# VectorE's order in the edge loop of a graph network: the add of an edge part between the two products of an older unit

## The chip, the cores and the metric

The kernel runs on one core of one Trainium2 chip. The time is that of one execution on the device, in microseconds (us), as the median of several runs. A profile of one more execution gives the rows quoted below. TensorE is PE in those rows (its weight loads are PEld), VectorE is DVE, ScalarE is ACT, GpSimd is POOL, SyncE is SP.

## The reference

One layer of a graph network on 6250 nodes with 256 features and 206250 edges (100000 pairs in both directions, and one loop for each node), sorted by target node. All data are fp32.

```python
h = relu(layernorm(x))                                   # no gain or bias here
polarity = clip(edge_attr[:, 0:1], 0, 1)
e = relu(edge_attr[:, 1:] @ W_e1.T + b_e1) @ W_e2.T + b_e2
edge_emb = (e * (polarity + 0.01)) @ W_le.T + b_le
msg = relu(h[src] + edge_emb)
aggr = segment_sum(msg, dst)
g = (h + aggr) @ W_g1.T + b_g1
out = x + relu(layernorm(g) * ln_g + ln_b) @ W_g2.T + b_g2
```

## The kernel before, in words

The host only lays the arrays out. A first phase normalises x and writes h + b_le to memory in HBM (`hb_d`). It also multiplies W_e2 by W_le into one matrix (`wc_s`, with the offset `bc_s`), so that each edge needs two matrix products: the first layer, and the edge part.

The edges go in **blocks** of 512 (403 of them), a block in two **units** of 256 edges (NU = 806 units, `u`), and two blocks, that is four units, in a **turn** (some 201). The program is written out in full, without a loop on the chip: Python loops place the instructions of each engine in the order in which they are issued, and no scheduler moves them. Every engine runs its own list in order and waits at semaphores for the others.

`forward(u)` places unit u:

- `edge_part(u)`: eight matmul records on TensorE (L326) into a PSUM bank `pz`, and then, on VectorE, the **add** (L332) `msg[u] = pz + bc_s`, which frees the bank. There are seven such banks, taken in a ring by all steps that need one; the matmul that takes a bank again waits for its last reader.
- in each unit with `u % 4 == 1`, `turn_of`: the **first layer** (L293) of the turn two further on, into four banks, which three relus on ScalarE (L309) and one operation on VectorE (L306) read; then the **sums** (L696), in which 0/1 matrices `sel` add the finished messages of a turn by target node on TensorE.

After `forward(u)` the loop over units places on VectorE one **piece** (`piece()`: a part of a `sel` matrix, L656, or a step of the node work, L793 or L231), and then the **products** of an older unit, `whole(made)`: for each half i of the unit `hg = msg * polarity + hg` (L678), where `hg` holds the rows of h that GpSimd gathered from `hb_d` (an indirect DMA, L627). A relu on ScalarE (L683) over the whole unit follows, and `hg` is then ready for the sums. How far `made` trails u is set by `lag`: 18 units at first, fewer as the loop goes on. In a unit with `u % 4 == 0` the lag is one larger, so that no product stands in it, and in the one after it, `u % 4 == 1`, two units' products do, behind the first layer. This holds for all but the first and last six turns (`by_two`).

After that, `due()` places at most one step of the **node work** in a unit with `u % 4` of 2 or 3: for each of the 49 windows of 128 nodes a transpose, a matrix product whose bank VectorE reads (L190), a layer normalisation (L152, L153, L158, L194), a second transpose that ScalarE reads (L204), a last product and the output (L218). ScalarE's L171 reads the first transpose.

`gathers(n)` places gathers up to unit n where they aren't placed yet; most are placed earlier, in step with TensorE, by `paced`. `add_pairs`, called as `sums`, places as many turns of sums as `made` allows, with three units (`LATER`) kept in between.

## Time and profile before

| | |
|---|---|
| median of three runs | 2539.52 us (2538.93 to 2548.43) |
| profiled execution | 2536.68 us, span 2534.7 us |
| TensorE busy | 2300.1 us, 91% of the span |
| VectorE busy | 1606.2 us, 63% |
| ScalarE busy | 1004.0 us, 40% |
| GpSimd busy | 1657.5 us, 65% |
| DMA | 330.25 MB, mean 130 GB/s |

A row of a group reads: line, engine, operation, written tile <- read tiles, shape, count | busy us, mean ns of one | idle us of the engine directly before such instructions, and what ended most of that. A row of waits reads: engine, tile and line that waited <- what ended the wait: us in total, times, the longest. A row of the timeline reads: start in us, us, the instruction, how many of them, and in brackets the idle time before it and what ended it. "issue" and "remote" stand for a wait whose end the profile shows no releaser for. A row of a window reads: its us, then busy us and count of PE, PEld, DVE, ACT and POOL, the granted clock of TensorE, the DMA share, and GB/s.

### The profile page before, as it was taken

How to read it: one execution, taken by the hardware profiler on the slowest of the kernel's cores; microseconds unless marked ns; L12 is line 12 of the kernel's file. 1: busy time of each engine (PE TensorE's matmuls, PEld its weight loads, DVE VectorE, ACT ScalarE, POOL GpSimd, SP SyncE). 2: the span in 40 equal slices, each digit the busy share in tenths (PEclk: the TensorE clock that was granted, in tenths of full speed). 3: DMA queues.
4: the chain of work that ended last, by engine and by line, in shares of the span. 5: the costliest groups of instructions: out<-in, count | busy, mean ns of one | idle time of the engine just before them, and what ended most of it. 6: DMA issues, size and time to landing. Idle time of an engine off the chain costs nothing.

```text
span 2534.7 us, 36092 instructions
## 1 busy us (share of the span) xinstructions
PE 2300.1 (91%) x11940; PEld 1573.7 (62%) x11940; DVE 1606.2 (63%) x3705; ACT 1004.0 (40%) x1804; POOL 1657.5 (65%) x1675
## 2 busy tenths in 40 slices
PE   9988999999989999899999999999999999899967
PEld 6665666566656666666666666666656666656645
DVE  7876666656666666566656665666666666656645
ACT  7433343333433344333434343334343433433422
POOL 7666666666666666666666666666666666666661
PEclk9999999999999999999999999999999999999988
DMA  9444443444444344444444444344444444443441
GB/s 309 140 122 134 132 129 116 127 137 124 129 129 131 116 131 135 133 119 127 136 132 130 118 129 136 116 127 137 130 122 128 133 136 121 129 133 116 119 125 38
DMA packets 176425, 330.25 MB, mean 130 GB/s; under 512 B 39056, under 2 KB 98281, under 8 KB 176233
## 3 DMA queue, kind: packets, MB, share of 16 engines
q0 software_dynamic: 77376, 211.39, 29.8%
q1 hardware_dynamic: 97556, 113.22, 13.8%
q10 hardware_dynamic: 1300, 3.28, 0.4%
q8 instruction: 95, 1.56, 0.3%
q14 instruction: 98, 0.79, 0.1%
HBM read 293.92 MB, written 33.82 MB: 129 GB/s over the span
## 4 chain that ended last, share of the span: by engine, by line
PE 81%; DVE 8%; issue 7%; another core or an unknown queue 2%; ACT 1%; DMA 0%; DVEq 0%; ACTq 0%; POOL 0%; POOLq 0%
PE pz L326 55%; PE pz L293 14%; PE pd L696 8%; DVE hg L678 2%; DVE msg L332 2%; PE pz L213 2%; PE pz L182 2%; DVE sel L656 1%; DVE st L152 0%; PE pz L167 0%; PE pz L200 0%; DVE e L306 0%; ACT hg L683 0%; ACT xt L433 0%
## 5 line engine op out<-in xcount | busy, mean ns | idle before, releaser
L627 POOL DMA_INDIRECT hg<-hb_d,src_s x1604 | 1612.6, 1005 | 808.3 <-issue 506.8
L326 PE MATMUL pz<-wc_s,e 128*128 128x256 f32 x6448 | 1578.8, 394 | 134.2 <-issue 120.9
L326 PEld LDWEIGHTS pz<-wc_s,e 128*128 128x128 f32 x6448 | 1235.2, 196 | 448.2 <-issue 236.7
L332 DVE TENSOR_TENSOR msg<-pz,bc_s 128x512 f32<-128x512 f32 x799 | 543.0, 686 | 733.2 <-PE pz L326 297.1
L683 ACT ACTIVATE hg<-hg 128x512 f32<-128x512 f32 x805 | 501.0, 629 | 997.9 <-DVE hg L678 827.0
L678 DVE SCALAR_TENSOR_TENSOR hg<-msg,pol_s,hg 128x256 f32<-128x256 f32 x1612 | 690.5, 478 | 10.1 <-DMA hg<-hb_d,src_s 5.3
L309 ACT ACTIVATE e<-pz,vecs 128x512 f32<-128x512 f32 x605 | 373.3, 684 | 243.4 <-remote 111.6
L293 PE MATMUL pz<-raw,we_s 64*128 64x512 f32 x1612 | 420.1, 626 | 40.2 <-DVE msg L332 24.9
L293 PEld LDWEIGHTS pz<-raw,we_s 64*128 64x128 f32 x1612 | 137.3, 186 | 223.3 <-issue 132.5
L696 PE MATMUL pd<-hg,sel 128*32 128x256 f32 x3216 | 241.0, 391 | 26.2 <-issue 25.3
L306 DVE TENSOR_SCALAR e<-pz,vecs 128x512 f32<-128x512 f32 x201 | 149.8, 745 | 137.9 <-remote 47.6
L696 PEld LDWEIGHTS pd<-hg,sel 128*32 128x32 f32 x3216 | 91.0, 110 | 226.9 <-issue 180.7
L656 DVE SCALAR_TENSOR_TENSOR sel<-iota_w,zero_c,rel 128x128 f32<-128x128 f32 x403 | 138.3, 343 | 0.0
L711 ACT ACTIVATE ms<-pd 128x256 f32<-128x256 f32 x66 | 25.4, 385 | 243.6 <-PE pz L326 101.6
L182 PE MATMUL pz<-wg_s,hT 128*128 128x256 f32 (+1 forms) x196 | 53.5, 387 | 12.3 <-issue 11.1
L213 PE MATMUL pz<-wg_s,nT 128*128 128x256 f32 (+1 forms) x196 | 51.5, 384 | 2.7 <-issue 1.8
L182 PEld LDWEIGHTS pz<-wg_s,hT 128*128 128x128 f32 (+1 forms) x196 | 37.0, 191 | 20.0 <-issue 13.1
L213 PEld LDWEIGHTS pz<-wg_s,nT 128*128 128x128 f32 (+1 forms) x196 | 37.2, 191 | 8.3 <-issue 2.1
L437 POOL TENSOR_TENSOR hb<-xt,rows_b 128x256 f32<-128x256 f32 (+1 forms) x49 | 34.1, 729 | 10.4 <-ACT xt L433 4.4
L204 ACT ACTIVATE nT<-pz,vecs 128x128 f32<-128x128 f32 (+1 forms) x98 | 38.8, 445 | 2.4 <-PE pz L200 2.4
L793 DVE TENSOR_TENSOR stb<-stb,ab 128x256 f32<-128x256 f32 x94 | 39.2, 417 | 0.0
L231 DVE SCALAR_TENSOR_TENSOR xt<-xt,zero_c,rows_b 128x128 f32<-128x128 f32 (+1 forms) x98 | 33.6, 344 | 0.0
(108 smaller groups left out, 379.9 us busy)
## 6 DMA issues: line engine op xcount, KB each, us to landing
raw<-in_raw_t_dram SPq DMA_DIRECT2D x202, 256.0 KB
hg<-hb_d,src_s POOLq DMA_INDIRECT x1604
sum_d<-zrow SPq DMA_DIRECT2D x94, 128.0 KB
ab<-sum_d SPq DMA_DIRECT2D x94, 128.0 KB
sum_d<-ms SPq DMA_DIRECT2D x264, 32.0 KB
hb_d<-hb SPq DMA_DIRECT2D x12, 512.0 KB
xt<-in_x_dram SPq DMA_DIRECT2D x48, 128.0 KB
out_dram<-ot SPq DMA_DIRECT2D x48, 128.0 KB
```

Source lines behind the costliest of these rows:

```text
L182: z = nc.tensor.matmul(ph[:n, 0, :], aT[:, c, :n], wg1_s[:, c, :], start=c == 0 and not bias_by_pe, stop=c == 1)
L213: z = nc.tensor.matmul(po[:n, 0, :], nT[:, c, :n], wg2_s[:, c, :], start=c == 0, stop=c == 1)
L293: z[c] = nc.tensor.matmul(pe[s, c], we1_s[s * F:(s + 1) * F, c * P:(c + 1) * P], raw[q][s * F:(s + 1) * F, :], start=True, stop=True)
L306: a = nc.vector.tensor_scalar(e1[b][:, c, :], pe[s, c], be1_s[:, c:c + 1], 0.0, op0=ALU.add, op1=ALU.max)
L309: a = nc.scalar.activation(e1[b][:, c, :], pe[s, c], AF.Relu, bias=be1_s[:, c:c + 1])
L326: last_z = nc.tensor.matmul(pz[:, i, :], e1[b][:, c, k:k + P], wc_s[:, c, :], start=c == 0, stop=c == 1)
L332: ps.read(nc.vector.tensor_add(msg[u], pz, bc_s))
L627: g = nc.gpsimd.indirect_dma_start(out=hg[u][:, i, :], out_offset=None, in_=hb_d, in_offset=bass.IndirectOffsetOnAxis(ap=src_s[:, 2 * u + ...
L656: nc.vector.scalar_tensor_tensor(sel[g][:, k * S:(k + 1) * S, :], iota_w.rearrange("p (o w) -> p o w", o=1).to_broadcast([P, S, W]), zero_ ...
L678: product = nc.vector.scalar_tensor_tensor(hg[u][:, i, :], m[:, i, :], pol_s[:, 2 * u + i:2 * u + i + 1], hg[u][:, i, :], op0=ALU.mult, op ...
L683: done[u] = product, nc.scalar.activation(hg[u], hg[u], AF.Relu)
L696: z = nc.tensor.matmul(acc[g][j * W:(j + 1) * W, :], sel[g][:, k * S + j, :], m[:, j % 2, :], start=k == 0, stop=b == blocks_of(g)[-1])
```

## The change

The add of unit u is placed between the two products of the older unit that is due in the same step of the loop (`half_of_products`, called ahead of the add and behind it). Before, both products came after the add, after a first layer where there is one, and after a piece. Only one older unit per step is split in this way (`eager`), and only where `by_two` holds. The second unit in a step with `u % 4 == 1` keeps its place behind the first layer, and `whole` now takes one more piece between its two products. The sums count as if the eager unit weren't made yet, so that they take the same turns as before.

```diff
@@ edge_part
             msg[u] = msg_p.tile([P, 2, D], F32, name="msg")
+            half_of_products(u, 0)
             if plain(u):
                 ps.read(nc.scalar.activation(msg[u], pz, AF.Copy))
             else:
                 ps.read(nc.vector.tensor_add(msg[u], pz, bc_s))
+            half_of_products(u, 1)
@@
-            def whole(u):
-
-                m = msg.pop(u)
+            def products(u, i):
+
+                if i == 0:
+                    opened(u)
+                product = nc.vector.scalar_tensor_tensor(hg[u][:, i, :], msg[u][:, i, :], pol_s[:, 2 * u + i:2 * u + i + 1],
+                                               hg[u][:, i, :], op0=ALU.mult, op1=ALU.add)
+                if u == NU - 1:
+                    nc.scalar.activation(hg[u][:, i, :], hg[u][:, i, :], AF.Relu)
+                elif i == 1:
+                    done[u] = product, nc.scalar.activation(hg[u], hg[u], AF.Relu)
+                if i == 1:
+                    msg.pop(u)
...
+            def whole(u, between=lambda: None):
+
+                products(u, 0)
+                between()
+                products(u, 1)
@@ add_pairs
-                while summed + pairs < NP and min(4 * (summed + pairs) + 4, NU) < made + last - (0 if last or summed > NP - 2 * FEW else LATER):
+                while summed + pairs < NP and min(4 * (summed + pairs) + 4, NU) < made - eager + last - (0 if last or summed > NP - 2 * FEW else LATER):
@@
+            def due_at(u):
+
+                lag = max(LEAST, LEAD - RAW - u // SHRINK) + (by_two(u // 4) and (u + 1) % 4 == TURN)
+                return min(u + 1 - lag, 5 * (u + 1 - LEAD) // 4)
+
+            def half_now(u, i):
+
+                nonlocal made, eager
+                if i == 0:
+                    eager = by_two(u // 4) and made < due_at(u)
+                    if eager:
+                        gathers(made + 1)
+                if eager:
+                    products(made, i)
+                    made += i
@@ the loop over units
-                lag = max(LEAST, LEAD - RAW - u // SHRINK) + (by_two(u // 4) and (u + 1) % 4 == TURN)
-                ready_for = min(u + 1 - lag, 5 * (u + 1 - LEAD) // 4)
-                while made < ready_for:
+                while made < due_at(u):
                     gathers(made + 1)
-                    whole(made)
+                    whole(made, piece)
                     made += 1
```

The lists of TensorE, GpSimd and SyncE keep their order from first to last; VectorE's and ScalarE's change. Below, an add is the row that writes `msg`, a product one that writes `hg` from `msg`, and the number in a name tells tiles apart (it differs between the two programs for the same tile). Line numbers shift: L332, L678, L656 and L683 of before are L333, L677, L659 and L682 after.

VectorE in the middle of the edge loop, from the add of a unit with `u % 4 == 2` to the add of the next one, in a turn with a node step (`hs`) between them. Before:

```order
L332 TENSOR_TENSOR msg_8186<-pz0_106,bc_s_69 128x512
L656 SCALAR_TENSOR_TENSOR sel_8006<-iota_w_77,zero_c_66,rel_72 128x128
L678 SCALAR_TENSOR_TENSOR hg_8103<-msg_7958,pol_s_71,hg_8103 128x256 x2
L190 TENSOR_TENSOR hs_8197<-pz1_107,rows_b_183 128x256
L152 BN_STATS st_8200<-hs_8197 128x6
L153 BN_AGGR mv1_8199<-st_8200 128x2
L158 RECIPROCAL rs1_8203<-rs1_8203 128x1
L194 TENSOR_SCALAR hs_8197<-hs_8197,mv1_8199,rs1_8203 128x256
L332 TENSOR_TENSOR msg_8250<-pz2_108,bc_s_69 128x512
```

And after:

```order
L677 SCALAR_TENSOR_TENSOR hg_8108<-msg_7958,pol_s_71,hg_8108 128x256
L333 TENSOR_TENSOR msg_8187<-pz0_106,bc_s_69 128x512
L677 SCALAR_TENSOR_TENSOR hg_8108<-msg_7958,pol_s_71,hg_8108 128x256
L190 TENSOR_TENSOR hs_8197<-pz1_107,rows_b_183 128x256
L152 BN_STATS st_8200<-hs_8197 128x6
L153 BN_AGGR mv1_8199<-st_8200 128x2
L158 RECIPROCAL rs1_8203<-rs1_8203 128x1
L194 TENSOR_SCALAR hs_8197<-hs_8197,mv1_8199,rs1_8203 128x256
L677 SCALAR_TENSOR_TENSOR hg_8125<-msg_7972,pol_s_71,hg_8125 128x256
L333 TENSOR_TENSOR msg_8250<-pz2_108,bc_s_69 128x512
```

One product now stands ahead of the first add, the next unit's first product ahead of the second add, and the piece that stood here (`sel`) has been taken earlier.

VectorE at a turn, from the add of the unit with `u % 4 == 1` to the add after the first layer (`e1` is L306's result). Before:

```order
L332 TENSOR_TENSOR msg_9196<-pz2_108,bc_s_69 128x512
L306 TENSOR_SCALAR e1_9202<-pz6_112,vecs_134 128x512
L656 SCALAR_TENSOR_TENSOR sel_9142<-iota_w_77,zero_c_66,rel_72 128x128
L678 SCALAR_TENSOR_TENSOR hg_9110<-msg_8946,pol_s_71,hg_9110 128x256 x2
L678 SCALAR_TENSOR_TENSOR hg_9119<-msg_8963,pol_s_71,hg_9119 128x256 x2
L332 TENSOR_TENSOR msg_9233<-pz0_106,bc_s_69 128x512
```

And after:

```order
L677 SCALAR_TENSOR_TENSOR hg_9110<-msg_8948,pol_s_71,hg_9110 128x256
L333 TENSOR_TENSOR msg_9197<-pz2_108,bc_s_69 128x512
L677 SCALAR_TENSOR_TENSOR hg_9110<-msg_8948,pol_s_71,hg_9110 128x256
L306 TENSOR_SCALAR e1_9206<-pz6_112,vecs_134 128x512
L659 SCALAR_TENSOR_TENSOR sel_9145<-iota_w_77,zero_c_66,rel_72 128x128
L677 SCALAR_TENSOR_TENSOR hg_9122<-msg_8965,pol_s_71,hg_9122 128x256 x2
L677 SCALAR_TENSOR_TENSOR hg_9160<-msg_8983,pol_s_71,hg_9160 128x256
L333 TENSOR_TENSOR msg_9234<-pz0_106,bc_s_69 128x512
```

The products of one of the two units have moved from behind L306 to both sides of the add, and one product of the unit after it has come in ahead of the last add.

ScalarE at the same turn (L683 or L682 is the relu of a unit, L309 those of the first layer). Before:

```order
L204 ACTIVATE nT_9177<-pz0_106,vecs_134 128x128 x2
L309 ACTIVATE e1_9201<-pz3_109,vecs_134 128x512
L309 ACTIVATE e1_9202<-pz4_110,vecs_134 128x512
L309 ACTIVATE e1_9201<-pz5_111,vecs_134 128x512
L683 ACTIVATE hg_9110<-hg_9110 128x512
L683 ACTIVATE hg_9119<-hg_9119 128x512
```

And after:

```order
L204 ACTIVATE nT_9178<-pz0_106,vecs_134 128x128 x2
L682 ACTIVATE hg_9110<-hg_9110 128x512
L309 ACTIVATE e1_9205<-pz3_109,vecs_134 128x512
L309 ACTIVATE e1_9206<-pz4_110,vecs_134 128x512
L309 ACTIVATE e1_9205<-pz5_111,vecs_134 128x512
L682 ACTIVATE hg_9122<-hg_9122 128x512
```

The relu of one unit has moved ahead of the three of the first layer.

## The prediction

> **What bounds the kernel now.** I read the page first, then the waits of TensorE's matmuls (PE) and of its weight loads (PEld), then stretches of the timeline. The profiled execution took 2536.68 us, of which the span is 2534.7; the median of the three timed runs is 2539.52 (2538.93 to 2548.43). I make the sum against 2536.68 and move the result to the median by the same difference. About 0.5%, or 12.7 us, is what a measurement of this kernel can tell from no change.

> ```profile
> PE 2300.1 (91%) x11940; PEld 1573.7 (62%) x11940; DVE 1606.2 (63%) x3705; ACT 1004.0 (40%) x1804; POOL 1657.5 (65%) x1675
> L326 PE MATMUL pz<-wc_s,e 128*128 128x256 f32 x6448 | 1578.8, 394 | 134.2 <-issue 120.9
> L332 DVE TENSOR_TENSOR msg<-pz,bc_s 128x512 f32<-128x512 f32 x799 | 543.0, 686 | 733.2 <-PE pz L326 297.1
> L683 ACT ACTIVATE hg<-hg 128x512 f32<-128x512 f32 x805 | 501.0, 629 | 997.9 <-DVE hg L678 827.0
> L678 DVE SCALAR_TENSOR_TENSOR hg<-msg,pol_s,hg 128x256 f32<-128x256 f32 x1612 | 690.5, 478 | 10.1 <-DMA hg<-hb_d,src_s 5.3
> L306 DVE TENSOR_SCALAR e<-pz,vecs 128x512 f32<-128x512 f32 x201 | 149.8, 745 | 137.9 <-remote 47.6
> ```

> TensorE is busy 2300.1 of 2534.7 us. VectorE (DVE) is busy 63%, and 733.2 us of its idle time stand directly before the adds of L332: it waits there for TensorE. A reordering on VectorE can win only what TensorE loses by waiting for VectorE, or for ScalarE (ACT), which waits 827.0 us for VectorE's products. That loss is small, as TensorE's own waits show (us in total, times, longest):

> ```profile
> PE pz L326 <- issue: 120.9, 193, 2.2
> PE pz L293 <- DVE msg L332: 24.9, 24, 2.5
> PE pz L326 <- DVE msg L332: 3.8, 6, 2.0
> PE pz L293 <- DVE hs L190: 2.5, 3, 1.0
> PE pz L326 <- ACT nT L204: 1.4, 5, 0.4
> PE pz L293 <- ACT hT L171: 0.3, 1, 0.3
> ```

> The largest wait, 120.9 us, has no releaser that the profile shows, and nothing here touches it. The five others add up to 24.9 + 3.8 + 2.5 + 1.4 + 0.3 = 32.9 us, 1.3% of the span: that is the whole prize. The weight loads show the same waits from the other side. A load often waits while an earlier matmul still runs, so these are upper bounds:

> ```profile
> PEld pz L293 <- DVE msg L332: 48.9, 52, 3.3
> PEld pz L326 <- DVE e L306: 7.5, 16, 0.9
> PEld pz L326 <- ACT nT L204: 6.7, 11, 0.9
> PEld pz L293 <- DVE hs L190: 6.2, 7, 1.9
> PEld pz L326 <- ACT e L309: 4.5, 10, 0.8
> PEld pz L293 <- ACT hT L171: 3.6, 6, 1.1
> ```

> How such a wait comes about is seen in one turn. I call a unit by its number modulo 4: after the first layer (L293) and the sums (L696), TensorE does units 2, 3, 0 and 1.

> ```profile
> 1152.10 0.69 DVE L332 TENSOR_TENSOR msg<-pz,bc_s 128x512 f32<-128x512 f32 x1 [3.48 <-PE pz L326]
> 1152.71 0.34 DVE L656 SCALAR_TENSOR_TENSOR sel<-iota_w,zero_c,rel 128x128 f32<-128x128 f32 x1
> 1152.76 1.13 PE L293 MATMUL pz<-raw,we_s 64*128 64x512 f32 x4
> 1152.97 0.88 DVE L678 SCALAR_TENSOR_TENSOR hg<-msg,pol_s,hg 128x256 f32<-128x256 f32 x2
> 1153.76 0.68 DVE L332 TENSOR_TENSOR msg<-pz,bc_s 128x512 f32<-128x512 f32 x1
> 1154.36 0.34 DVE L656 SCALAR_TENSOR_TENSOR sel<-iota_w,zero_c,rel 128x128 f32<-128x128 f32 x1
> 1154.50 1.13 PE L293 MATMUL pz<-raw,we_s 64*128 64x512 f32 x4 [0.61 <-DVE msg L332]
> 1154.62 0.87 DVE L678 SCALAR_TENSOR_TENSOR hg<-msg,pol_s,hg 128x256 f32<-128x256 f32 x2
> 1155.53 0.63 ACT L683 ACTIVATE hg<-hg 128x512 f32<-128x512 f32 x1 [1.02 <-DVE hg L678]
> 1156.06 0.79 ACT L204 ACTIVATE nT<-pz,vecs 128x128 f32<-128x128 f32 x2
> 1156.27 0.68 DVE L332 TENSOR_TENSOR msg<-pz,bc_s 128x512 f32<-128x512 f32 x1
> 1156.75 1.84 ACT L309 ACTIVATE e<-pz,vecs 128x512 f32<-128x512 f32 x3
> 1156.91 1.35 PE L326 MATMUL pz<-wc_s,e 128*128 128x256 f32 x5 [0.28 <-issue]
> ```

> VectorE waits 3.48 us for unit 2. From then on it runs back to back: add 2 at 1152.10, a piece, two products, add 3 at 1153.76, a piece, two products. TensorE's first layer needs the bank that add 3 reads and stands 0.61 us. ScalarE's relu (L683) needs the last product, L204 stands behind it, ends at 1156.85, and TensorE goes on at 1156.91 after 0.28 us.

> The steps in this stretch, from start to start: an add holds VectorE 0.60 us (1153.76 to 1154.36), a piece 0.26 (1152.71 to 1152.97), a product 0.395 (1152.97 to 1153.76, halved).

> **The change part by part.** It adds no work: 1612 products, 799 adds and 805 relus stay, each with its duration. TensorE's, GpSimd's and SyncE's rows keep their order, so no DMA is passed. It moves products and pieces.

> *Unit 2 to add 3.* Before: add, piece, product, product, add 3: 0.60 + 0.26 + 0.79 = 1.65 us. After: add, second product, piece, first product of the next unit, add 3: again 1.65. One product has left for the 3.48 us wait, and another has come in ahead of add 3. The 24.9 us of L293 on L332 therefore stay, except where the piece is gone. Each turn now takes a second piece between the two products behind the first layer, so later slots are sometimes empty; each saves 0.26 us. Bounds: nothing, or 24 waits x 0.26 = 6.2 us. I take 1 us, since most slots still hold a piece.

> *What hangs on the products of unit 3.* The relu of unit 3 starts one product (0.395 us) earlier, and 0.26 more where the piece of unit 3 now stands behind the product. L204 and L171 behind it come 0.4 to 0.65 us earlier, more than the 0.28 us that TensorE stood here. Lower bound: the PE rows, 1.4 + 0.3 = 1.7 us. Upper bound: the PEld rows, 6.7 + 3.6 = 10.3 us. I take 5 us: the place above stood 0.28 us but its gap goes under "issue" in the PE rows, so these rows undercount, and 17 waits x 0.28 is 4.8.

> *Node steps between units 2 and 3.* In such turns L190 stands behind the products of unit 2:

> ```profile
> 1032.84 0.42 DVE L190 TENSOR_TENSOR hs<-pz,rows_b 128x256 f32<-128x256 f32 x1
> 1033.32 1.13 PE L293 MATMUL pz<-raw,we_s 64*128 64x512 f32 x4 [0.56 <-issue]
> 1035.04 0.67 DVE L332 TENSOR_TENSOR msg<-pz,bc_s 128x512 f32<-128x512 f32 x1
> 1035.77 2.43 PE L326 MATMUL pz<-wc_s,e 128*128 128x256 f32 x10 [0.32 <-issue]
> ```

> After the change L190 has neither the first product nor the piece ahead of it: 0.65 us earlier, more than the 0.56. But the next add (1035.04) has a product put in front of it, so it gains only the piece's 0.26, and TensorE's second gap (0.32) waits for that add. Bounds: nothing, or 7 waits (PEld on L190) x 0.65 = 4.6 us. I take 2, near 7 x 0.26.

> *Costs in the turn.* The add of unit 1 now has a product on each side, so L306 comes 0.395 us later. Its 16 PEld waits give at most 16 x 0.4 = 6.4 us, and no PE row names it: I take 1 us. On ScalarE a relu now stands ahead of the three L309. Here it could start when the second product ends: 1156.27 + 0.60 + 0.48 = 1157.35; it takes 0.63, and the L309 start at 1157.98 instead of 1156.75, 1.23 us later. Ten PEld waits of 4.5 us exist; I take 1 us more, between nothing and 10 x 1.23 = 12.3.

> *Products ahead of adds.* A product that waits for its gathered rows now holds an add behind it. The trace has such a case, in a place where the product already stood ahead:

> ```profile
> 161.07 0.48 DVE L678 SCALAR_TENSOR_TENSOR hg<-msg,pol_s,hg 128x256 f32<-128x256 f32 x1 [1.32 <-DMA hg<-hb_d,src_s]
> 162.21 1.99 PE L326 MATMUL pz<-wc_s,e 128*128 128x256 f32 x8 [0.79 <-DVE msg L332]
> ```

> All products together wait 5.3 us for gathers, so they mostly find their rows there; but they now come a wait earlier. Bounds: nothing to 5.3 us; I take 2.

> Sum: -1 - 5 - 2 + 1 + 1 + 2 = -4 us. The profiled execution would take 2532.7, the median 2535.5.

> I count nothing for the clock. It falls after some gaps of TensorE, as here, where a gap of 1.64 us ended just ahead of a stretch at 0.50:

> ```profile
> 1100.96 0.38 PE L326 MATMUL pz<-wc_s,e 128*128 128x256 f32 x1 [1.64 <-issue]
> 1101.45:1108.28 6.83, 5.93 (x14) 4.90 (x15) 5.27 (x14) 2.62 (x6) 4.23 (x5) 0.50 0.46 118
> ```

> The gaps that I expect to close are a fifth to a third of that, so I leave the clock to the lower end: one such stretch less is 3.4 us. [...]

> **The rivals.** *TensorE's waits for VectorE go (faster).* For it: the products leave for VectorE's idle time, so every signal finds VectorE free, and shorter gaps spare slow stretches. Against it: the row of unit 2 to add 3 is as long as before. The whole 32.9 us give 2506.6; half of it, which I take as its time, 2523.

> *ScalarE becomes late (slower).* The L309 free the banks of the first layer, and they now stand behind a relu that stands behind the second product and the add of unit 1. The bank of the first L309 is claimed again seven banks on: with two node steps among them that is unit 0, two units after 1156.91, and at 1.99 us each (eight matmuls at 162.21) no sooner than 1160.9. The first L309 would end near 1157.98 + 0.61 = 1158.6. So 2.3 us are left here; beyond that TensorE waits. If one turn in three (201 turns, by L306) went over by 0.5 us, that is 33 us: 2572. [...] Against this rival: ScalarE is 40% busy.

> *Gathers become late (slower).* Were 30 adds held by 0.45 us each, that is 13.5 us: 2553. Against it stand the 5.3 us.

> *It does nothing.* Only idle time of VectorE and ScalarE is filled in another order: 2539.5.

> **How the numbers follow.** Forecast 0.50, no effect 0.13, TensorE's waits go 0.20, ScalarE late 0.10, gathers late 0.07. The forecast and no effect lie within 0.5% of 2539.5 (2526.8 to 2552.2): 0.63. Faster: 0.20. Slower: 0.17. My terms' best ends together give -6.2 - 10.3 - 4.6 = -21.1, their worst ends +6.4 + 12.3 + 5.3 = +24, which cannot well meet. The range 2522 to 2554 holds the forecast, no effect, the late gathers and about half of the faster rival; left out are 0.10 and 0.10.

> **What would show it.** Right: the waits of L293 on L332 stay near 25 us, those on L204, L171 and L190 shrink or vanish, VectorE's idle time before the adds falls by about the products moved into it, and waits on L309 stay small. Wrong: L326 or L293 waiting tens of us for L309 or L306 (the second rival), products with tens of us of idle time from gathers (the third), or L293 on L332 down to half (the first).

## The result, and the profile after

The changed kernel took 2537.51 us (median of 20 runs, 2531.37 to 2545.16) and the kernel before 2539.4 us (20 runs, 2532.51 to 2548.43) on the same chip. The ratio is 0.9991, with a 95% interval of 0.9980 to 1.0001. The forecast was 2535.5 us and no measurable change. The profiled execution took 2531.37 us, of which the span is 2529.4; before it was 2536.68 and 2534.7.

From the page of the changed kernel (L333, L677 and L682 are the former L332, L678 and L683):

```profile
PE 2304.9 (91%) x11940; PEld 1572.5 (62%) x11940; DVE 1606.6 (64%) x3705; ACT 991.5 (39%) x1804; POOL 1664.9 (66%) x1675
L326 PE MATMUL pz<-wc_s,e 128*128 128x256 f32 x6448 | 1571.6, 393 | 127.2 <-issue 114.1
L333 DVE TENSOR_TENSOR msg<-pz,bc_s 128x512 f32<-128x512 f32 x799 | 548.7, 687 | 680.3 <-remote 298.5
L682 ACT ACTIVATE hg<-hg 128x512 f32<-128x512 f32 x805 | 506.5, 631 | 1246.2 <-DVE hg L677 732.4
L677 DVE SCALAR_TENSOR_TENSOR hg<-msg,pol_s,hg 128x256 f32<-128x256 f32 x1612 | 744.4, 478 | 22.8 <-DMA hg<-hb_d,src_s 17.5
L306 DVE TENSOR_SCALAR e<-pz,vecs 128x512 f32<-128x512 f32 x201 | 150.3, 748 | 164.3 <-remote 86.3
```

The work is the same. VectorE's idle time before the adds fell from 733.2 to 680.3 us. Half of that stands elsewhere now: before L306 it rose from 137.9 to 164.3 us, and the products' waits for gathered rows rose from 5.3 to 17.5 us. The waits of TensorE and of its weight loads (us in total, times, longest):

```profile
PE pz L326 <- issue: 114.1, 194, 2.4
PE pd L711 <- issue: 44.7, 74, 1.7
PE pz L293 <- DVE msg L333: 14.4, 12, 2.2
PE pz L326 <- DVE msg L333: 7.6, 11, 1.2
PE pz L293 <- DVE hs L190: 1.2, 3, 0.5
```

```profile
PEld pz L293 <- DVE msg L333: 32.7, 36, 3.0
PEld pz L293 <- DVE hs L190: 5.3, 7, 1.3
PEld pz L326 <- DVE e L306: 4.1, 9, 0.8
PEld pz L293 <- ACT hT L171: 2.3, 4, 0.9
PEld pz L326 <- ACT e L309: 1.7, 3, 0.8
PEld pz L326 <- ACT nT L204: 1.2, 3, 0.4
```

L326's wait for L204 is gone. Added up over all rows of the first list (only its longest rows are shown), the matmuls stood 53.9 us for VectorE and ScalarE before and 28.9 us after: 25 us less. But the rows named "issue", which have no releaser, rose from 169.5 to 183.4 us, those before the sums (now L711) from 25.3 to 44.7 us. So in these two profiles 13.9 of the 25 us turn up again elsewhere on TensorE.

One turn of the changed kernel, VectorE and the first layer (start and duration in us; in brackets the idle time ahead):

```profile
1153.40 0.69 DVE L333 TENSOR_TENSOR msg<-pz,bc_s 128x512 f32<-128x512 f32 x1 [1.88 <-PE pz L326]
1154.01 0.47 DVE L677 SCALAR_TENSOR_TENSOR hg<-msg,pol_s,hg 128x256 f32<-128x256 f32 x1
1154.40 0.34 DVE L659 SCALAR_TENSOR_TENSOR sel<-iota_w,zero_c,rel 128x128 f32<-128x128 f32 x1
1154.67 0.48 DVE L677 SCALAR_TENSOR_TENSOR hg<-msg,pol_s,hg 128x256 f32<-128x256 f32 x1
1156.30 0.69 DVE L333 TENSOR_TENSOR msg<-pz,bc_s 128x512 f32<-128x512 f32 x1 [1.16 <-PE pz L293]
1157.05 1.13 PE L293 MATMUL pz<-raw,we_s 64*128 64x512 f32 x4 [1.58 <-issue]
```

The order is as the prediction laid it out: add 2, product, piece, product, add 3. Here VectorE stood idle for 1.16 us before add 3, waiting for TensorE; the first layer then stood 1.58 us, until add 3 ended at 1156.99. By the profile the matmuls that fill the bank of add 3 had ended at 1154.41, 1.9 us before the add began. The trace has the update of the semaphore on which that add waits at 1156.28. So this stop hung on that signal, and not on VectorE's order.

### The profile page after: what moved, and what is told of

Read it like the earlier page. It is cut to its first block, busy times and chain, and to the rows that moved or that the text cites. A ratio compares the mean times of both kernels' runs of the same rounds, so it can differ in the third digit from the quotient of the medians.

```text
span 2529.4 us, 36095 instructions
## 1 busy us (share of the span) xinstructions
PE 2304.9 (91%) x11940; PEld 1572.5 (62%) x11940; DVE 1606.6 (64%) x3705; ACT 991.5 (39%) x1804; POOL 1664.9 (66%) x1675
## 3 DMA queue, kind: packets, MB, share of 16 engines
q0 software_dynamic: 77376, 211.39, 28.7%
## 4 chain that ended last, share of the span: by engine, by line
PE 82%; issue 9%; DVE 5%; another core or an unknown queue 1%; DMA 1%; ACT 1%; POOL 0%; SPq 0%; DVEq 0%; POOLq 0%; ACTq 0%
PE pz L326 55%; PE pz L293 13%; PE pd L711 9%; PE pz L213 2%; PE pz L182 2%; DVE msg L333 2%; DVE hg L677 2%; DMA hg<-hb_d,src_s 0%; PE pz L200 0%; PE pz L167 0%; DVE sel L659 0%; POOL hg L630 0%; DVE hs L194 0%; ACT hg L682 0%
## 5 line engine op out<-in xcount | busy, mean ns | idle before, releaser
L326 PE MATMUL pz<-wc_s,e 128*128 128x256 f32 x6448 | 1571.6, 393 | 127.2 <-issue 114.1
L326 PEld LDWEIGHTS pz<-wc_s,e 128*128 128x128 f32 x6448 | 1228.3, 195 | 437.7 <-issue 235.7
L682 ACT ACTIVATE hg<-hg 128x512 f32<-128x512 f32 x805 | 506.5, 631 | 1246.2 <-DVE hg L677 732.4
L333 DVE TENSOR_TENSOR msg<-pz,bc_s 128x512 f32<-128x512 f32 x799 | 548.7, 687 | 680.3 <-remote 298.5
L677 DVE SCALAR_TENSOR_TENSOR hg<-msg,pol_s,hg 128x256 f32<-128x256 f32 x1612 | 744.4, 478 | 22.8 <-DMA hg<-hb_d,src_s 17.5
L293 PE MATMUL pz<-raw,we_s 64*128 64x512 f32 x1612 | 414.6, 621 | 26.8 <-DVE msg L333 14.4
L309 ACT ACTIVATE e<-pz,vecs 128x512 f32<-128x512 f32 x605 | 372.1, 679 | 86.7 <-remote 41.0
L711 PE MATMUL pd<-hg,sel 128*32 128x256 f32 x3216 | 259.6, 391 | 46.1 <-issue 44.7
L293 PEld LDWEIGHTS pz<-raw,we_s 64*128 64x128 f32 x1612 | 137.9, 186 | 202.5 <-issue 143.6
L711 PEld LDWEIGHTS pd<-hg,sel 128*32 128x32 f32 x3216 | 94.1, 109 | 261.7 <-issue 218.8
L306 DVE TENSOR_SCALAR e<-pz,vecs 128x512 f32<-128x512 f32 x201 | 150.3, 748 | 164.3 <-remote 86.3
L659 DVE SCALAR_TENSOR_TENSOR sel<-iota_w,zero_c,rel 128x128 f32<-128x128 f32 x403 | 139.2, 346 | 0.0
L204 ACT ACTIVATE nT<-pz,vecs 128x128 f32<-128x128 f32 (+1 forms) x98 | 38.7, 445 | 3.1 <-PE pz L200 2.4
```

The costliest lines, as they stand in the source:

```text
L293: z[c] = nc.tensor.matmul(pe[s, c], we1_s[s * F:(s + 1) * F, c * P:(c + 1) * P], raw[q][s * F:(s + 1) * F, :], start=True, stop=True)
L306: a = nc.vector.tensor_scalar(e1[b][:, c, :], pe[s, c], be1_s[:, c:c + 1], 0.0, op0=ALU.add, op1=ALU.max)
L309: a = nc.scalar.activation(e1[b][:, c, :], pe[s, c], AF.Relu, bias=be1_s[:, c:c + 1])
L326: last_z = nc.tensor.matmul(pz[:, i, :], e1[b][:, c, k:k + P], wc_s[:, c, :], start=c == 0, stop=c == 1)
L333: ps.read(nc.vector.tensor_add(msg[u], pz, bc_s))
L659: nc.vector.scalar_tensor_tensor(sel[g][:, k * S:(k + 1) * S, :], iota_w.rearrange("p (o w) -> p o w", o=1).to_broadcast([P, S, W]), zero_ ...
```

## Experiments

Twelve kernels ran, four at a time beside the kernel before, each four on a chip of their own. The kernel before took 2503.39 us on the chip of e1 to e4 (called the second below), 2161.82 on that of e5 to e8 (the third) and 2502.9 on that of e9 to e12 (the fourth). The first is the one of the result above; the record does not number it, and that it is a chip of its own is taken from its time. Ratios are to the kernel before on the same chip.

**Parts of the change: e1_no_piece and e2_piece_only.** The first takes the second piece out of the changed kernel, the second adds it alone to the kernel before.

```diff
-                    whole(made, piece)
+                    whole(made)
```

> The change without its second piece: the add still stands between the two products, but products behind the first layer again follow each other without a piece between. In the profile of the changed kernel the first layer's matmuls (L293) stand 14.4 us for the adds, against 24.9 us before. Theory A (the moved products and the moved pieces each carry part of that, and all of it is small): the slots between add 2 and add 3 hold a piece again, so L293 on the add goes back up to 17 to 23 us, L204 and L171 stay gone since the relu still comes a product earlier, and the time lies 1 to 5 us above the changed kernel. Rival B (the fall from 24.9 to 14.4 us is the doing of the moved product alone): L293 on the add stays at 13 to 16 us and the time within 2 us of the changed kernel. Rival C (such differences are chance between one execution and the next): L293 on the add anywhere, with no order between the kernels.

> The kernel before with only the second piece: both products of a unit stay behind the add, with a piece between them. Theory A: later slots are empty more often, L293 on the add falls from 24.9 to 17 to 23 us, the waits on L204 and L171 stay (1.7 us), the time is 0 to 3 us below before. Rival B (the moved product alone did it): L293 on the add stays near 25 us, the time within 2 us of before. Rival C: no order between the kernels.

Measured: e1 2505.4 us, ratio 1.0014 (1.0005 to 1.0023); e2 2501.69 us, ratio 0.9999 (0.9990 to 1.0008). TensorE's waits in e1:

```profile
PE pz L326 <- issue: 101.6, 170, 2.4
PE pz L293 <- DVE msg L333: 21.3, 17, 2.7
```

and in e2:

```profile
PE pz L293 <- DVE msg L332: 23.2, 20, 3.0
PE pz L326 <- ACT nT L204: 5.7, 10, 0.8
```

L293 on the add fits theory A in e1 and lies just above its upper edge of 23 us in e2, but the changed kernel itself had 23.1 us in a later run (e9) against 14.4 in the first. So this row as it stands can't be put down to either part (rival C); the table further down, which leaves out the time in which VectorE itself stood idle, gives an order (14.0 us in e1, 17.5 in e2, 18.1 before, 10.2 and 11.9 in the changed kernel) that fits theory A, but the differences are hardly larger than the scatter. Steadier is L326's row of L204: 5 times before, 10 times in e2 where the products were not moved, absent in the changed kernel, e1 and e9. The changed kernel did not run on this chip, so how far e1's time lies from it stays open.

**More on the same line: e3_clear and e4_loaded.** In the steps of units 2 and 3, e3 places all four products and a piece ahead of add 2; e4 places the four products between add 2 and add 3. The core of e4, with `i == 0` and a `piece()` ahead of the loop in e3, which then has none behind add 2:

```diff
+                if by_two(u // 4) and u % 4 in (2, 3):
+                    if u % 4 == 2 and i == 1:
+                        while made < due_at(u + 1) and made < u:
+                            gathers(made + 1)
+                            whole(made)
+                            made += 1
+                    return
```

> The changed kernel, but in the steps of units 2 and 3 all four products and the piece stand ahead of add 2, where VectorE waits for TensorE, and nothing but a node step stands between add 2 and add 3. Theory A (what TensorE loses to VectorE hangs on the length from add 2 to add 3, which the change left at 1.65 us): that length falls to 0.60 us, L293 on the add falls from 14.4 to under 6 us, and the time lies 6 to 14 us below the changed kernel. Rival B (the order on VectorE is worth nothing, because the adds wait for TensorE's own signals): L293 on the add stays within 4 us of 14.4, the time within 3 us. Rival D (products ahead of adds wait for their gathered rows): products' waits for gathers rise from 17.5 to over 40 us, and the time to above the changed kernel's by 3 to 12 us.

> The other way round: in the steps of units 2 and 3 all four products stand between add 2 and add 3, which come 0.60 + 4 x 0.395 = 2.18 us apart, with the piece 2.4 us, against 1.65 us. Theory A: each of the some 20 to 40 turns in which VectorE runs back to back lengthens by 0.5 to 0.8 us, L293 on the add rises from 14.4 to 30 to 60 us, and the time by 12 to 35 us. Rival B (order without effect): L293 on the add under 20 us, the time within 3 us of the changed kernel.

Measured: e3 2512.66 us, ratio 1.0033 (1.0019 to 1.0048); e4 2502.14 us, ratio 0.9998 (0.9989 to 1.0007). Rows of e3, then of e4:

```profile
PE pz L326 <- issue: 117.5, 187, 2.4
PE pz L293 <- DVE msg L333: 17.2, 9, 11.1
DVE hg L677 <- DMA hg<-hb_d,src_s: 91.6, 116, 2.9
```

```profile
PE pz L326 <- issue: 83.7, 141, 1.7
PE pz L293 <- DVE msg L333: 47.4, 33, 8.2
PE pd L711 <- issue: 22.8, 34, 2.2
```

Theory A foresaw e4's wait (30 to 60 us) and failed on its time (12 to 35 us more). With waits for VectorE and ScalarE at 76.5 us in all, against 42.0 in e1 on the same chip, e4 was as fast as before. In e3 the number of stops on the add fell to 9, one of them of 11.1 us, and the time still rose. VectorE's order did not make that long stop:

```profile
2448.68 0.69 DVE L333 TENSOR_TENSOR msg<-pz,bc_s 128x512 f32<-128x512 f32 x1 [15.48 <-remote]
2449.52 1.23 PE L293 MATMUL pz<-raw,we_s 64*128 64x512 f32 x2 [11.05 <-DVE msg L333]
```

The profile puts TensorE's stop down to the add, but VectorE had itself stood idle for 15.48 us ahead of that add, for a signal whose sender the profile does not name. Rival D's two numbers came true there (gather waits over 40 us, 3 to 12 us slower); its mechanism did not show, since TensorE stood only 33.7 us for VectorE and ScalarE.

**The rivals of the prediction: e5_changed_again, e6_relu_twice, e7_clear_early, e8_half_gathers.** e5 is the changed kernel; e6 runs each relu twice; e7 is e3 with gathers further ahead; e8 drops each unit's second gather.

```diff
+                    nc.scalar.activation(hg[u], hg[u], AF.Relu)     # e6
-AFLOAT = 6.0                                                        # e7
+AFLOAT = 12.0
+                if i == 1:                                          # e8, in gather()
+                    return
```

> The changed kernel as it is, on the same chip as the other runs of this call. In the first four runs the kernel before took 2503.39 us here, against 2539.4 where the change was first measured. Theory A' (VectorE's order moves TensorE's waits about, but the time hardly): ratio to before 0.998 to 1.0015, so 2498 to 2507 us; L293 on the add 12 to 25 us, the issue waits of L326 100 to 120 us. Rival (the change is worth more on this chip, where stops without a releaser are shorter and VectorE's waits weigh more): ratio under 0.997.

> The changed kernel with every relu of a unit (L682) run twice, which leaves the result as it is: some 800 more ScalarE instructions of 0.63 us, 506 us of work, and L309, L204 and L171 up to 0.63 to 1.26 us later in each turn. The prediction's second rival held that the banks freed by L309 have about 2.3 us left. Theory A' (ScalarE has that slack): waits of TensorE on L309, L204 and L171 stay under 10 us, the time within 5 us of the changed kernel. Rival (ScalarE is near its limit behind the new order): those waits rise to 30 us or more, and the time by 20 us or more.

> The kernel with all four products ahead of add 2 (2512.66 us, products' waits for gathers 91.6 us in 116 places) with its gathers allowed to run 12 instead of 6 us of TensorE's work ahead, about 4.7 gathers earlier. Theory G (its loss of 0.33% came from products that waited for gathers ahead of adds): those waits fall under 20 us and the time comes back to 2498 to 2506 us. Rival H (the loss came from TensorE's own stops and the clock: 53 of 716 windows of 3.41 us at half clock there, 35 where the products stood between the adds): the waits for gathers fall, but the time stays above 2508 us.

> The changed kernel without the second gather of every unit; its second product adds the first one's rows instead, so that half of the gathered rows are left out of the result. VectorE, ScalarE and TensorE do the same work. GpSimd loses 800 issues, the DMA engines 106 of 330 MB. TensorE's longest waits have no releaser in the profile; in the raw records they come in runs of three to eight matmuls that start 0.7 to 1.4 us apart instead of 0.216. Theory S (TensorE's instructions or its signals are held up by the traffic of transfers): the issue waits of L326 fall from 114 to under 70 us, half-clock windows fall too, and the time falls by 25 to 80 us. Rival T (these stops are TensorE's own, from whatever else): issue waits stay at 90 to 120 us and the time within 8 us of the changed kernel.

Measured: e5 2163.62 us, ratio 1.0007 (0.9998 to 1.0016); e6 2165.75, 1.0017 (1.0008 to 1.0026); e7 2167.41, 1.0027 (1.0016 to 1.0038); e8 2160.2, 0.9991 (0.9982 to 1.0000). On this chip the kernel before took 14% less time than on the second (2161.82 against 2503.39 us). From the page of e5:

```profile
PE 2144.8 (99%) x11940; PEld 1535.7 (71%) x11940; DVE 1644.3 (76%) x3705; ACT 991.2 (46%) x1804; POOL 1629.0 (75%) x1675
L326 PE MATMUL pz<-wc_s,e 128*128 128x256 f32 x6448 | 1479.4, 383 | 3.9 <-DVE msg L333 3.9
L677 DVE SCALAR_TENSOR_TENSOR hg<-msg,pol_s,hg 128x256 f32<-128x256 f32 x1612 | 746.6, 478 | 76.6 <-DMA hg<-hb_d,src_s 74.6
```

TensorE is busy 99% of the span, its matmuls have no wait named "issue", and they stand 9.4 us in all for VectorE and ScalarE. Where nothing else stops TensorE, less than 10 us are left to win from these waits, and the change brought nothing (the kernel before was not profiled on this chip). The absolute times and the wait rows of e5's expectation did not hold, its ratio did.

e6 gave ScalarE 1479.9 - 991.2 = 488.7 us more work and cost 2165.75 - 2163.62 = 2.1 us, less than the two intervals can tell from nothing. The matmuls' whole wait for L309 was

```profile
PE pz L326 <- ACT e L309: 1.2, 3, 0.6
```

so the rival "ScalarE becomes late" is out on this chip, with more than the change's own delay put on it; in the changed kernel's profile on the first chip L309 held TensorE once, for 0.3 us. In e7 the products waited 211.0 us for rows, 282 times, and not under 20 us as theory G had it. e7 and e3 ran on different chips, so their times don't decide between G and H. But e7 lost 0.27% at a granted clock of 0.999 with 0.4 us of "issue" waits, so on this chip the loss needs neither TensorE's own stops nor the clock. TensorE stood 14.4 us for VectorE and ScalarE there against 9.4 in e5, and took 3.8 us longer; its longest such stop, 2.3 us, was for an add behind products that had waited 0.73 and 0.84 us for their rows. In e8 the waits for rows went from 74.6 us to

```profile
DVE hg L679 <- DMA hg<-hb_d,src_s: 2.8, 3, 1.1
```

and the time fell by 2163.62 - 2160.2 = 3.4 us: 71.8 us of waits on VectorE were worth at most 5% of their length, since e8 also took away 802 gathers and 105 MB of transfers. That prices the rival "gathers become late" on this chip. Theories S and T stay undecided, since this chip had none of the stops they speak of.

**Is a wait for VectorE paid? e9_changed_third, e10_loaded_again, e11_loaded_more, e12_clear_again.** e9 is the changed kernel, e10 is e4, e12 is e3 (with gathers 6 us ahead as in e3; the 12 us in its expectation are not what ran). e11 adds idle work between add 2 and add 3 of e4:

```diff
+                        for _ in range(6):
+                            nc.vector.scalar_tensor_tensor(idle, msg[u][:, 0, :P], pol_s[:, 2 * u:2 * u + 1],
+                                                           msg[u][:, 1, :P], op0=ALU.mult, op1=ALU.add)
```

> The changed kernel, beside the three that follow, all on one chip. The kernel before took 2539.4, 2503.4 and 2161.8 us on three chips so far: on the first two TensorE stood some 200 us in stops without a releaser and ran 5 to 7% of its windows at half clock, on the third neither was there. Theory A' (VectorE's waits trade with those other stops): ratio to before 0.998 to 1.002 on whatever chip. Rival: outside that.

> Again the kernel with four products between add 2 and add 3 (2.18 us and more from one to the other). Theory A' : on a chip with stops, L293 on the add 35 to 60 us against 12 to 25 us in the changed kernel, the issue waits of L326 and of the sums lower by 30 to 60 us than in the changed kernel, time within 3 us of it. On a chip without stops, L293 on the add under 10 us and the time within 4 us. Rival W (a wait for VectorE is paid in full): the time lies above the changed kernel's by as much as the waits on the add do, 20 us or more on a chip with stops.

> The same with six more VectorE instructions (128x128, some 0.26 us each from start to start, into a scratch tile) between add 2 and add 3, which then come about 4.0 us apart; VectorE gets some 310 us of work more, which leaves the result as it is. Theory A': there is an end to the trade: once the wait on add 3 is longer than what the other stops leave open, it is paid. On a chip with stops L293 on the add rises to 120 to 250 us, and the time by 20 to 100 us above the kernel with four products there. On a chip without stops VectorE goes from 76% to about 90% busy and the time rises by 5 to 60 us. Rival V (VectorE's order and load are worth nothing at all here): within 4 us of the kernel with four products.

> The kernel with all four products ahead of add 2 and 12 us of gathers ahead, beside the others on one chip. It was 0.27% above before where TensorE was 99% busy and the products waited 211.0 us for their rows; with gathers at 6 us ahead it was 0.33% above on another chip. Theory A': L293 on the add under 10 us, the products' waits for gathers over 60 us, the time 0.1 to 0.4% above before. Rival B (no effect): within 0.1% of before.

Measured: e9 2505.03 us, ratio 1.0005 (0.9992 to 1.0019); e10 2502.74, 1.0003 (0.9993 to 1.0012); e11 2508.94, 1.0026 (1.0017 to 1.0035); e12 2508.79, 1.0024 (1.0015 to 1.0033). TensorE's waits in e9:

```profile
PE pz L326 <- issue: 119.7, 210, 1.7
PE pd L711 <- issue: 24.9, 45, 1.7
PE pz L293 <- DVE msg L333: 23.1, 16, 4.8
```

in e10:

```profile
PE pz L326 <- issue: 78.5, 132, 2.2
PE pz L293 <- DVE msg L333: 57.4, 33, 12.2
PE pd L711 <- issue: 16.8, 31, 1.6
```

and in e11:

```profile
PE pz L293 <- DVE msg L333: 77.3, 58, 4.7
PE pz L326 <- issue: 31.9, 56, 2.2
PE pz L326 <- DVE msg L333: 27.1, 20, 2.5
PE pz L293 <- DVE hs L190: 23.8, 16, 3.3
PE pd L712 <- issue: 3.9, 7, 1.7
```

Added up over all rows of each list:

| kernel (chip) | waits for VectorE, ScalarE | "issue" waits | both | L293 on the add; VectorE's own part | time |
|---|---|---|---|---|---|
| before (first) | 53.9 | 169.5 | 223.4 | 24.9; 18.1 | 2539.4 |
| changed (first) | 28.9 | 183.4 | 212.3 | 14.4; 10.2 | 2537.51 |
| e3 clear (second) | 33.7 | 172.8 | 206.5 | 17.2; 5.6 | 2512.66 |
| e1 no piece (second) | 42.0 | 160.2 | 202.2 | 21.3; 14.0 | 2505.4 |
| e2 piece only (second) | 48.5 | 148.3 | 196.8 | 23.2; 17.5 | 2501.69 |
| e4 loaded (second) | 76.5 | 131.2 | 207.7 | 47.4; 30.7 | 2502.14 |
| e12 clear (fourth) | 28.7 | 173.2 | 201.9 | 15.0; 10.3 | 2508.79 |
| e9 changed (fourth) | 38.8 | 162.9 | 201.7 | 23.1; 11.9 | 2505.03 |
| e10 loaded (fourth) | 88.1 | 117.8 | 205.9 | 57.4; 40.1 | 2502.74 |
| e11 loaded more (fourth) | 170.8 | 59.9 | 230.7 | 77.3; 74.6 | 2508.94 |
| e5 changed (third) | 9.4 | 0.0 | 9.4 | 0.0; 0.0 | 2163.62 |

VectorE's own part is what is left of these stops when the time is taken out in which VectorE executed nothing, as in the stop of 11.1 us in e3. Read in this way, the row rises with the work between add 2 and add 3: 5.6 and 10.3 us with none, 10.2 to 18.1 with two products and at times a piece, 30.7 and 40.1 with four products, 74.6 with six more instructions. On each of the three chips with stops, the longer TensorE stands for VectorE and ScalarE, the shorter are the "issue" waits. Each row is one execution.

From e9 to e10 the waits for VectorE and ScalarE rose by 49.3 us and the "issue" waits fell by 45.1; the time did not rise. To e11 they rose by 132.0 us, the "issue" waits fell by 103.0, and the time rose by 3.9 us, 3% of the added waits. Without the stops in which the engine waited for was itself idle (14.6 us in e9, 22.3 in e10, 10.0 in e11) the waits still rose by 41.6 and 136.6 us, so the trade does not come from such stops. Rival W is refuted. Theory A' had the trade right and overrated its end: it gave e11 a time 20 to 100 us above e10's, and it was 6.2 (rival V's bound was 4); L293 on the add reached 77.3 us and not 120. e12 repeats e3: gather waits 92.1 us, ratio in A's band, L293 on the add 15.0 us and not under 10.

## Why the prediction was right or wrong

No measurable change was forecast, and on three chips the ratio was 0.9991, 1.0007 and 1.0005. The 4 us that the sum gave are not to be seen: on the first chip the medians differ by 1.9 us, on the two others the sign is the opposite. "It does nothing", with a chance of 0.13, fits the times as well as the forecast did. So the hit on the number says little for the sum: its terms were smaller than what these runs can tell apart, and the main step behind them, that a wait removed is time gained, did not hold on the first chip.

- *L293 on the add stays, -1.* The row reads 14.4 and 23.1 us in two profiles of the changed kernel, 21.3 without the piece, 23.2 with the piece alone. The first profile by itself would have spoken for the rival "TensorE's waits go"; the row differs by 8.7 us between two profiles of one kernel (on two chips), most of the 10.5 us by which it fell. VectorE's own part of it reads 18.1 us before and 10.2 and 11.9 after: 6 to 8 us less, where the sum took 1 with an upper bound of 6.2. So the term was rather too small, though this part too differs by 4.7 us between e3 and e12, which are one program; and no gain in time shows.
- *L204 and L171, -5.* The waits went as worked out: the two PE rows from 1.7 us to none, their PEld rows from 10.3 to 3.5. But no gain in time shows.
- *L190, -2.* 2.5 to 1.2 us on the PE rows, 0.8 in e9: the direction holds, at the low end.
- *L306 and L309, +1 and +1.* No cost: their PEld rows fell from 7.5 and 4.5 to 4.1 and 1.7 us. e6 shows how far from the limit ScalarE was.
- *Gathers, +2.* The waits rose by 12.2 us, more than twice the upper bound of 5.3 us that I took from the row of before. The price was bounded rightly all the same: e8 gained 3.4 us by 71.8 us of them, on the third chip.
- *VectorE's idle time before the adds.* The sign given for it, a fall by about the products moved into it, was wrong: some 570 products of 0.395 us moved ahead of an add, and the fall was 52.9 us. VectorE's idle time as a whole hardly changed (span less busy time, 928.5 us before and 922.8 after).
- *The prize of 32.9 us.* The sum leaves out rows of the same list that were not shown, such as 5.9 us for L793's result (once) and 3.3 for the relu L683; with all rows the prize was 53.9 us. And here the working failed, by the step "The largest wait, 120.9 us, has no releaser that the profile shows, and nothing here touches it". VectorE's order touches it strongly: 119.7, 78.5 and 31.9 us in e9, e10 and e11. Each of my terms took a wait for VectorE as paid in full; on the fourth chip about 3% was (e11).
- *The clock.* I left it out of the sum. In the raw clock records the half-clock time was 182.9 us before and 164.1 after, and 157.0, 154.8 and 167.2 in e9 to e11. It does not follow the waits for VectorE. On the second and fourth chips it is longest in the two kernels with products ahead of add 2: 195.0 us in e3 and 173.9 in e12, against 137.0 to 167.2 in the others. The granted clock over all their runs is lower too: on average 0.964 in e3 and 0.963 in e12, and 0.969 to 0.971 in every other kernel on the same two chips.

Shown is the trade, on the fourth chip and in the same order on the second: added stops at VectorE take the place of stops without a releaser, for most of their length (45.1 of 49.3 us, 103.0 of 132.0). The rest of the 132.0 us is met by busy time, which falls from 2292.1 us in e9 to 2264.7 in e11. Why is open. In the raw records many of the stops without a releaser come in bursts: three or more matmuls that start 0.6 to 2.6 us apart instead of 0.216 (the median step of TensorE's matmuls in the profiles before and after), 31 times with 126 us in e9, 26 times with 98 us in e10, 5 times with 28 us in e11, never on the third chip. My two guesses, a limit on TensorE's mean rate and a slow supply of its instructions that catches up while it waits, are shown by no run: the one made to tell them apart (e8) met a chip without such stops. One simple form of the second is unlikely: the bursts do not go with the transfers of the queue that the page calls q8, instruction (95 packets in a run). Of 264 bursts in ten profiles, 140 start in the first half of the interval between two of these transfers and 124 in the second. Nor is it settled why the kernels with products ahead of add 2 are 0.24 to 0.33% slower. On the second and fourth chips a lower granted clock goes with it, on the third late rows do; neither was tested as the cause.

## What to carry to other kernels

Before a wait is priced, look at what else stops the same engine: where it also stands some 170 us without a releaser, a wait removed may only move there. A wait row of some 20 us read 14.4 and 23.1 us in two profiles of one program here. Look whether the engine that is blamed was itself idle during the stop: in e3 that was so for most of a row. Judge a part of a change by rows that vanish or triple, and by ratios over many runs. The cheapest test of a claimed bottleneck is to make it worse: e11's longer stops at VectorE said more than any attempt to shorten them.

## What the runs showed of the hardware

Chips differ far more than the kernels here: the same program took 2539.4, 2503.4, 2502.9 and 2161.8 us on what are taken for four chips, with a mean granted clock of 0.964 in the profile of the first and 0.998 in that of the changed kernel on the fastest.

```profile
987.08 0.38 PE L182 MATMUL pz<-wg_s,hT 128*128 128x256 f32 x1 [0.92 <-issue]
988.54 0.38 PE L326 MATMUL pz<-wc_s,e 128*128 128x256 f32 x1 [1.08 <-issue]
989.95 0.58 PE L326 MATMUL pz<-wc_s,e 128*128 128x256 f32 x1 [1.03 <-issue]
```

```profile
982.00:985.40 3.40, 3.40 (x29) 2.09 (x26) 0.12 (x1) 0.00 (x0) 2.60 (x3) 1.00 0.62 205
985.40:988.80 3.40, 1.40 (x6) 0.71 (x4) 0.00 (x0) 1.26 (x2) 2.68 (x3) 1.00 0.38 102
988.80:995.60 6.80, 4.96 (x13) 3.95 (x13) 4.24 (x11) 2.22 (x4) 3.07 (x4) 0.50 0.32 98
```

TensorE was idle 2.0 of 3.4 us in the second stretch, in pieces of about 1 us, and the next 6.8 us ran at 0.50. In the 3.41 us directly ahead of each of the 34 stretches at 0.50, TensorE ran no matmul for 1.98 us in the median; ahead of the 34 in the changed kernel on the same chip it was 1.90 us. In the stretches of the same length at full clock that were followed by full clock (655 and 659) it was 0.20 and 0.19 us on average. No run changed TensorE's idle time alone, so that it sets the clock is not shown.

On the fast chip the gathers' issues on GpSimd run almost without a break: in e5 they are busy 1584.2 us, with 492.6 us of idle time directly ahead of them, together 2076.8 of 2161.8 us. Here are the first and the last of ten in a row.

```profile
999.93 1.16 POOL L630 DMA_INDIRECT hg<-hb_d,src_s  x1 [0.30 <-issue]
1011.80 0.96 POOL L630 DMA_INDIRECT hg<-hb_d,src_s  x1 [0.30 <-issue]
```

Nine steps in 11.87 us are 1.32 us each. Over the whole run the 1604 gathers start 1.29 us apart on average, from 65.7 to 2137.6 us of a span of 2161.8, and 99% of the steps are under 1.6 us. The shortest step in the profiles before and after, on the first chip, is 1.25 and 1.24 us. So by these numbers GpSimd left hardly any room for a wider allowance (e7) to bring them earlier there.
